# A pre-norm attention layer on one core: layer norm statistics from the loaded blocks instead of a second load, and another order at the end of the last slice

## The chip, the cores and the metric

The kernel runs on one core of a Trainium2 chip. The metric is the device time in microseconds (us) of one execution. Before the change the median of three runs is 2884.72 us (2884.47 to 2885.43). The engines are named as in the profile: PE is TensorE, with PEld for its weight loads; DVE is VectorE, ACT is ScalarE, POOL is GpSimd and SP is SyncE, which issues nearly all transfers (DMAs).

## The reference

```python
h = jnp.maximum(_layernorm(x, axis=-1), 0.0)          # x: (128, 128, 768), eps 1e-5
x = x + _L0_gnn_ref(h, adj, Wq, bq, Wk, bk, Wv, bv, beta)

# in _L0_gnn_ref: 12 heads of 64
q = _split_heads(input_graph @ Wq + bq)                # k and v alike
scores = jnp.einsum('bhqd,bhkd->bhqk', q, k) / jnp.sqrt(HD)
scores = scores + beta * adj_e                         # adj_e = adj[:, None]
scores = jnp.where(adj_e > 0, scores, -9e15)
probs = jax.nn.softmax(scores, axis=-1)
out = jnp.einsum('bhqk,bhkd->bhqd', probs, v)
```

There are 128 graphs of 128 nodes with 768 features. Each graph is normed row by row, projected to queries, keys and values, and attends within itself where its adjacency is positive. The attention's output is added to x. All is float32.

## The kernel before

The graphs go through the core in 32 groups (G = 0 to 31) of four. For each group the kernel makes three projections, called slices: `qk0` (queries and keys of heads 0 to 5), `v` (all values) and `qk1` (queries and keys of heads 6 to 11). A slice is not a plain product of blocks: the list `PRODUCTS` names 15 products of sums of activation blocks (`A..`, `S..`) with sums of weight blocks (`B..`, `T..`), and what each adds to or takes from which output block. A product is one call of `product` (L355) with eight matmul instructions, 16 records in the trace. Each product belongs to one of four chains (a, b, c, d); a chain has one PSUM bank, in which its products accumulate one after another. After each product the bank is read, by ACT (L392) where it is the first for its output block, otherwise by a DVE addition (L396 for q and k, L382 and L387 for v). The next product of the same chain writes that bank again, so it has to wait until it has been read. There are eight banks in a queue `free`; `take` and `give` move them in order.

The loop over G writes out by hand what else is done after which product: `then(n, f)` puts f behind product n of the slice that is being built. In this way the attention of one group runs inside the slices of its own and the next group. `scores` (L406) follows product 1 of a slice: it makes three pairs of score blocks in six banks, each read by DVE with the bias (L421) and then exponentiated by ACT (L424). `attend` (L443) multiplies with the values (L452), takes reciprocals of the sums, and divides (L429 to L436); POOL adds x (L457) and SP stores. The order on each engine's queue is set by a scheduler from these calls; `issue_after` (in `behind`, `behind_scores` and others) forbids it to place a step ahead of a named one.

The next group G+1 is prepared meanwhile. Its x is loaded in blocks of 32 nodes by 192 features (`load_x`, L151), into tiles that come free when the previous group's blocks have been transposed (`to_hT`, L310, L315), which happens in the qk1 slice. ACT norms the blocks in place (`norm`, L304, L308) during the v slice, with a scale `rstd` and a shift for each.

Layer norm statistics come in two ways. In group 0's and group 1's loop turns (so for groups 1 and 2) `stats` (L225, L230) takes them from the x blocks on DVE, 16 per group. A row's 768 features lie on four partitions there, so `moments_1` (L235) sums the means over partitions with two small matmuls on PE (L241), four records, in a bank of its own, then DVE makes deviations (L244 to L248), `moments_2` (L251) does the same for the variances (L255 to L260), and POOL takes the power -1/2 and the shift (L262, L264). The bank is held for three products. From G = 2 on, that is for groups 3 to 31, the rows are loaded a second time instead, as whole rows in two halves (`load_halves`, L271), into tiles that share their places with `adj` and `adjT`; DVE takes statistics of 384 features (`row_stats`, L283, L284), `row_moments` (L286) finishes them with two DVE and two POOL instructions and sends them to the blocks' partitions by 16 transfers of 1 KB (L299). `load_adj` (L324), `bias_1` (L332) and `bias_2` (L348) make the bias from adjacency: a transposition, a mask, a product, a fill of the tile on POOL, a predicated copy, a square on ACT and a maximum.

The last group's qk1 slice has its own order of products (`LAST`) and half blocks of attention (`scores_half`, L460; `attend_half`, L481; arguments: head pair, then which two graphs), named here (5,0), (4,0), (3,0), (3,1), (5,1), (4,1). `scores_half` loads x for the residual, makes the scores (L472), bounds and biases them (L476) and exponentiates (L479). `attend_half` multiplies with the values (L489) and hands on `store`: division, residual addition (L497) and the store (L499). For (4,1) the `store` waits in the list `stores` until `over` (L742) has been computed from all divisors; `over` decides, by a small matmul (L744) and a reduction (L745), if the slow general path has to run.

Of the kernel before, what the change touches and what calls it, by code (L numbers as in the profile page):

```python
# [17 lines left out]
P = 128  # L18
# [96 lines left out]
def direct(ctx, tc, x, adj, wq, bq, wk, bk, wv, bv, beta, out, bad):  # L115
# [153 lines left out]
    rows = {}  # L269

    def load_halves(G, g):  # L271

        for h in range(2):
            t = rows[G, g, h] = work.tile([P, VH], F32, tag=("adj", "adjT")[h], name=f"half_{G}_{g}_{h}", bufs=1)
            nc.sync.dma_start(t, x[G * GRP + g, :, h * VH:(h + 1) * VH])

    def row_stats(G, g):

        if g == 0:
            rows[G] = stat.tile([P, GRP, 2, nc.vector.BN_STATS_DIM], F32, tag="strow", name=f"strow_{G}", bufs=1)  # L280
            rows[G, "mv"] = stat.tile([P, GRP, nc.vector.BN_AGGR_DIM], F32, tag="mvrow", name=f"mvrow_{G}", bufs=1)
        for h in range(2):
            nc.vector.bn_stats(rows[G][:, g, h, :], rows[G, g, h])  # L283
        nc.vector.bn_aggr(rows[G, "mv"][:, g, :], rows[G][:, g])  # L284

    def row_moments(G):  # L286

        mv = rows[G, "mv"]
        ve = stat.tile([P, GRP], F32, tag="verow", name=f"verow_{G}", bufs=1)
        nc.vector.tensor_scalar(ve, mv[:, :, 1], EPS, None, op0=ALU.add)  # L290
        mean = stat.tile([P, GRP], F32, tag="meanrow", name=f"meanrow_{G}", bufs=1)
        nc.vector.tensor_scalar(mean, mv[:, :, 0], -1.0, None, op0=ALU.mult)
        t = stat.tile([P, 2, GRP], F32, tag="row2", name=f"row2_{G}", bufs=1)
        nc.gpsimd.tensor_tensor(t[:, 0], ve, nhalf.to_broadcast([P, GRP]), ALU.pow)
        nc.gpsimd.tensor_tensor(t[:, 1], mean, t[:, 0], ALU.mult)
        to = stat.tile([P, NB, 2, GRP], F32, tag="block2", name=f"block2_{G}", bufs=1)
        for b in range(NB):
            for a in range(NB):
                nc.sync.dma_start(to[a * SQ:(a + 1) * SQ, b], t[b * SQ:(b + 1) * SQ])  # L299
        for g in range(GRP):  # L300
            for b in range(NB):
                rstd[G, g * NB + b], shift[G, g * NB + b] = to[:, b, 0, g:g + 1], to[:, b, 1, g:g + 1]

# [156 lines left out]
    def scores_half(G, oc, r):  # L460
# [14 lines left out]
        for i in range(2):  # L475
            nc.vector.scalar_tensor_tensor(e[:, i], ps[i][:, 0:2 * N].rearrange("p (g n) -> p g n", g=2), SCORE_CAP * ISCALE, biasT[G][:, 2 * r:2 * r + 2, :],  # L476
                                           op0=ALU.min, op1=ALU.add)
            give(ps[i])
            nc.scalar.activation(e[:, i], e[:, i], AF.Exp, scale=1.0 / ISCALE)  # L479

    def attend_half(G, oc, r):  # L481
# [11 lines left out]
        def store():  # L493
            divide()
            give(bank)
            t = xo[G, oc, r]
            nc.vector.tensor_add(t, t, o.rearrange("p (b j) d -> p b (j d)", j=2))  # L497
            g0 = G * GRP + 2 * r
            nc.sync.dma_start(out[g0:g0 + 2, :, oc * P:(oc + 1) * P].rearrange("g n d -> n g d"), t)  # L499

        if r == 1 and oc == 4:
            stores.append(store)
        else:
            store()
# [52 lines left out]
    def rows_1(g):  # L557

        t = xg[0, g].rearrange("p b f -> p (b f)")
        s = stat.tile([P, 2, nc.vector.BN_STATS_DIM], F32, tag="strow_0", name=f"strow0_{g}", bufs=2)  # L560
# [5 lines left out]
        mv = stat.tile([P, nc.vector.BN_AGGR_DIM], F32, tag="mvrow_0", name=f"mvrow0_{g}", bufs=2)  # L566
        nc.vector.bn_aggr(mv, s)
        ve = stat.tile([P, 1], F32, tag="verow_0", name=f"verow0_{g}", bufs=2)
# [77 lines left out]
    early, raw = [], []  # L646
    for G in range(NG):
# [4 lines left out]

        def behind(f, *args):

            with tc.issue_after(added[G].ins):
                return f(*args)
# [4 lines left out]
        if G + 1 < NG:  # L661
            for g in range(GRP):
                then(6, lambda g=g: load_x(G + 1, g, (nc.sync,)))
                if G == 1:
                    then(11 + g, lambda g=g: behind_scores(stats, G + 1, g))
                elif G:
                    then((0, 5, 8, 11)[g], lambda g=g: load_halves(G + 1, g))
                    then((4, 7, 10, 13)[g], lambda g=g: behind(row_stats, G + 1, g))
            if G > 1:
                raw = []  # L670
                then(14, lambda: raw.append(load_adj(G + 1)))
                then(14, lambda: row_moments(G + 1))
# [17 lines left out]
        if G + 1 < NG:  # L690
            got = []
            at = 3 if G else 5
            for g in range(GRP):
                if not G:
                    then(g, lambda g=g: stats(G + 1, g))
                then(at + 5 + g, lambda g=g: behind(norm, G + 1, g) if G > 1 else norm(G + 1, g))
            if G < 2:
                then(at, lambda: got.extend(moments_1(G + 1, 0, GRP * NB)))
                then(at + (3 if G else 2), lambda: moments_2(G + 1, 0, GRP * NB, *got[:2]))
            if G:  # L700
                then(8, lambda: got.append(behind(bias_1, G + 1, raw.pop()) if raw else bias_1(G + 1, load_adj(G + 1))))
                then(12, lambda: bias_2(G + 1, got[-1]))
# [29 lines left out]
        for at, f, *args in (  # L732
            (0, load_xo, 0), (0, load_xo, 1), (0, load_xo, 2), (0, attend, 0), (2, attend, 2), (4, attend, 1),
            (9, scores_half, 5, 0), (10, scores_half, 4, 0), (11, attend_half, 5, 0), (12, scores_half, 3, 0),
            (12, attend_half, 4, 0), (13, scores_half, 3, 1), (13, attend_half, 3, 0), (14, scores_half, 5, 1),
            (14, attend_half, 3, 1), (14, scores_half, 4, 1), (14, attend_half, 5, 1), (14, attend_half, 4, 1),
        ):
            then(at, lambda f=f, args=args: f(G, *args))
        slice_of(G, "qk1", todo, LAST)
# [138 lines left out]
```

## Time and profile before

| what | value |
| --- | --- |
| median of 3 runs | 2884.72 us |
| the profiled execution's own time | 2884.47 us |
| its span, first to last instruction | 2882.7 us |
| granted TensorE clock | 0.999 |
| start of the qk1 slice of groups 1, 2, 3 | 164.79, 253.96, 343.13 us |
| L283, statistics of half rows (DVE) | 232 instructions, 118.2 us, 549 ns each |
| L230, statistics of a block (DVE) | 40 instructions, 344 ns each |
| L294, power for a group's rows (POOL) | 29 instructions, 1017 ns each |
| L262, power for a group's blocks (POOL) | 2 instructions, 2908 ns each |
| L457, residual addition 128x512 (POOL) | 189 instructions, median 1.27 us |
| L497, residual addition 128x256 (DVE) | 6 instructions, 423 ns each |

A timeline line gives start and duration in us, engine, line of the kernel, operation, the tile written and those read, the shapes and the number of records; in brackets the idle time before it and what ended that. Matmul records overlap each other, so the distance from one start to the next says what a matmul costs the queue, and its duration does not.

### The profile page before, as it was taken

The numbers are of one execution on the slowest core, as the hardware profiler recorded it, in microseconds if no ns is written. First come the engines' busy times: TensorE is split into PE (matmuls) and PEld (weight loads), VectorE is DVE, ScalarE is ACT, GpSimd is POOL, SyncE is SP. The second block draws the span as 40 slices with busy tenths as digits, with TensorE's granted clock in tenths as the row PEclk, the third lists the DMA queues.
The fourth block names the chain that finished last, engine by engine and source line by source line (L and its number), as shares of the span: only waits on it lengthen the run. The fifth ranks groups of instructions, "written<-read, shape, count | busy, mean of one in ns | idle before, by whom it ended". The sixth has DMA issues, their size and how long they took to land.

```text
span 2882.7 us, 81559 instructions
## 1 busy us (share of the span) xinstructions
PE 2872.4 (100%) x35330; PEld 2014.5 (70%) x35330; DVE 1955.9 (68%) x4511; ACT 806.5 (28%) x1750; POOL 316.9 (11%) x304
## 2 busy tenths in 40 slices
PE   9999999999999999999999999999999999999999
PEld 7666677666677676776667766677666677666776
DVE  7866666666666666666766666666666666666665
ACT  2422322232222323313232132322223222322221
POOL 1111111111011010110101101011101111110110
PEclk9999999999999999999999999999999999999999
DMA  6222233222232222322223322233222232222311
GB/s 167 77 62 76 58 84 87 73 71 67 75 88 80 64 74 68 87 86 63 76 65 86 90 60 82 60 85 88 69 75 62 80 88 75 69 70 72 88 41 39
DMA packets 413467, 218.31 MB, mean 76 GB/s; under 512 B 110384, under 2 KB 412720, under 8 KB 413104
## 3 DMA queue, kind: packets, MB, share of 16 engines
q1 hardware_dynamic: 411232, 212.66, 26.8%
q8 instruction: 277, 4.54, 0.6%
q10 hardware_dynamic: 1872, 0.40, 0.1%
q14 instruction: 86, 0.70, 0.1%
HBM read 162.14 MB, written 50.33 MB: 74 GB/s over the span
## 4 chain that ended last, share of the span: by engine, by line
PE 99%; DVE 1%; issue 0%; POOL 0%; POOLq 0%
PE bank L371 85%; PE bank L417 6%; PE bank L452 6%; PE bank L533 1%; PE bank L595 0%; DVE A L315 0%; DVE qk_T L206 0%; DVE qk L396 0%; DVE S L321 0%; DVE e L421 0%; PE bank L472 0%; PE bank L489 0%; PE bank L584 0%; DVE e L476 0%; DVE xo L497 0%
## 5 line engine op out<-in xcount | busy, mean ns | idle before, releaser
L371 PE MATMUL bank<-S,qk_T 128*64 128x256 f32 x7056 | 822.5, 379 | 0.8 <-ACT qk L392 0.8
L396 DVE TENSOR_TENSOR qk<-qk,bank 128x512 f32<-128x512 f32 x630 | 426.6, 677 | 411.8 <-PE bank L371 406.3
L371 PEld LDWEIGHTS bank<-S,qk_T 128*64 128x64 f32 x7056 | 503.8, 137 | 256.1 <-ACT e L424 5.2
L392 ACT ACTIVATE qk<-bank,bqk 128x256 f32<-128x256 f32 x756 | 315.8, 469 | 1149.3 <-PE bank L371 962.8
L457 POOL TENSOR_TENSOR xo<-xo,o 128x512 f32<-128x512 f32 x189 | 253.5, 1342 | 2075.2 <-DVE o L436 1777.9
L371 PE MATMUL bank<-S,qk_B 128*64 128x256 f32 x4032 | 478.2, 379 | 1.0 <-DVE qk L396 1.0
L371 PE MATMUL bank<-A,qk_T 128*64 128x256 f32 x4032 | 478.6, 379 | 0.4 <-DVE qk L396 0.4
L371 PE MATMUL bank<-v_T,S 128*64 128x256 f32 x3584 | 421.8, 380 | 0.0
L424 ACT ACTIVATE e<-e 128x512 f32<-128x512 f32 x378 | 227.8, 628 | 642.8 <-DVE e L421 641.8
L371 PEld LDWEIGHTS bank<-A,qk_T 128*64 128x64 f32 x4032 | 284.3, 137 | 137.0 <-DVE qk L396 0.5
L387 DVE TENSOR_TENSOR v<-v,bank 128x512 f32<-128x512 f32 x320 | 219.8, 687 | 232.6 <-PE bank L371 230.8
L371 PEld LDWEIGHTS bank<-S,qk_B 128*64 128x64 f32 x4032 | 278.6, 137 | 128.9 <-DVE qk L396 1.4
L371 PEld LDWEIGHTS bank<-v_T,S 128*64 128x64 f32 x3584 | 254.7, 137 | 130.4 <-issue 5.7
L421 DVE SCALAR_TENSOR_TENSOR e<-bank,biasT 128x512 f32<-128x512 f32 x378 | 231.7, 682 | 109.1 <-PE bank L417 109.1
L371 PE MATMUL bank<-v_B,S 128*64 128x256 f32 x2048 | 243.2, 379 | 0.0
L371 PE MATMUL bank<-v_T,A 128*64 128x256 f32 x2048 | 237.9, 379 | 0.0
L308 ACT ACTIVATE x<-x,block 128x192 f32<-128x192 f32 x464 | 217.3, 535 | 39.9 <-DMA block<-row 39.1
L452 PEld LDWEIGHTS bank<-v,e 128*64 128x64 f32 x6048 | 208.6, 138 | 27.3
L315 DVE STREAM_TRANSPOSE A<-x 128x256 f32<-128x256 f32 x378 | 211.8, 612 | 4.0 <-ACT x L308 4.0
L452 PE MATMUL bank<-v,e 128*64 128x65 f32 x6048 | 208.3, 221 | 0.0
L382 DVE TENSOR_TENSOR v<-bv_b,bank 128x512 f32<-128x512 f32 x192 | 131.8, 687 | 105.2 <-PE bank L371 105.2
L371 PEld LDWEIGHTS bank<-v_B,S 128*64 128x64 f32 x2048 | 147.1, 137 | 73.9
(90 smaller groups left out, 1603.6 us busy)
## 6 DMA issues: line engine op xcount, KB each, us to landing
x<-in_x_dram SPq DMA_DIRECT2D x504, 96.0 KB, 2.6
xo<-in_x_dram SPq DMA_DIRECT2D x189, 256.0 KB, 3.0
out_dram<-xo SPq DMA_DIRECT2D x189, 256.0 KB, 2.6
half<-in_x_dram SPq DMA_DIRECT2D x232, 192.0 KB, 2.8
adj<-in_adj_dram SPq DMA_DIRECT2D x128, 64.0 KB, 3.0
block<-row SPq DMA_DIRECT2D x464, 1.0 KB, 1.7
qk_T<-in_L_gnn_Wq_dram SPq DMA_DIRECT2D x10, 128.0 KB, 3.7
qk_T<-in_L_gnn_Wk_dram SPq DMA_DIRECT2D x10, 128.0 KB, 3.8
```

The costliest lines, as they stand in the source:

```text
L308: nc.scalar.activation(t, t, AF.Relu, bias=shift[G, n], scale=rstd[G, n])
L315: last = nc.vector.transpose(t[:, :, g * N:(g + 1) * N].rearrange("p c (b i) -> p c b i", i=SQ), src)
L371: nc.tensor.matmul(p[q:q + HD, i, :], lhs[:, q:q + HD], rhs, start=(first and i == 0 and c == 0), stop=(c == 1), skip_group_check=True)
L382: added[G] = nc.vector.tensor_tensor(o4, bias[:, None, :, :].to_broadcast([P, 2, 4, HD]), p.rearrange("p g (h d) -> p g h d", d=HD), ALU.a ...
L387: added[G] = nc.vector.tensor_tensor(o, o, got, ALU.add if sign > 0 else ALU.subtract)
L392: nc.scalar.activation(t[:, i, :], p[:, i, :], AF.Identity, bias=bqk[:, i, oc:oc + 1], scale=float(sign))
L396: added[G] = nc.vector.tensor_tensor(t, t, p, ALU.add if sign > 0 else ALU.subtract)
L417: nc.tensor.matmul(ps[oc, i][k:k + HD, g * N:(g + 1) * N], t[r, 1, at][:, k:k + HD], t[r, 0, at], start=True, stop=True)
L421: taken[0] = nc.vector.scalar_tensor_tensor(e, ps[oc, i].rearrange("p (g n) -> p g n", g=GRP), SCORE_CAP * ISCALE, biasT[G], op0=ALU.min, ...
L424: nc.scalar.activation(e, e, AF.Exp, scale=1.0 / ISCALE)
L452: nc.tensor.matmul(pa[q:q + HD, 2 * g + i, :], es[G, oc, i][:, 2 * r + g, q:q + HD], vt[G, "v", r, h // 4][:, 4 * g + h % 4, :], start=Tru ...
L457: nc.gpsimd.tensor_add(t, t, o.rearrange("p a (b j) d -> p (a b) (j d)", j=2))
```

## The change

In the main loop the second way of taking statistics is removed: `load_halves`, `row_stats`, `row_moments` and the ordering helper `behind` go. All groups from 3 on now take `stats`, `moments_1` and `moments_2` like groups 1 and 2. In the loop's text `stats` stand behind products 11 to 14 of the qk0 slice, without an order after the scores; `moments_1` stand behind product 3 and `moments_2` behind product 6 of the v slice; the adjacency is loaded where `bias_1` is called. As built, the scheduler places the 16 `bn_stats` of group G+1 in the qk1 slice of group G-1, between its last additions, and the bias's DVE work in the following qk0 slices.

In the last slice the scores of (5,1) stand behind product 13 instead of 14; the divisions, additions and stores of all three `r == 1` blocks go into `stores`; that of (3,1) is taken out first and ordered after the last score sums; those of (5,1) and (4,1) follow `over`. The additions of (3,1) and (5,1) go to POOL. Some tags of the first group's statistics tiles are renamed.

```diff
-    def load_halves(G, g):
...
-    def row_stats(G, g):
...
-    def row_moments(G):
...
+            taken[0] = nc.vector.scalar_tensor_tensor(e[:, i], ps[i][:, 0:2 * N].rearrange("p (g n) -> p g n", g=2),
+                                                      SCORE_CAP * ISCALE, biasT[G][:, 2 * r:2 * r + 2, :],
+                                                      op0=ALU.min, op1=ALU.add)
...
-            nc.vector.tensor_add(t, t, o.rearrange("p (b j) d -> p b (j d)", j=2))
+            engine = nc.gpsimd if r == 1 and oc != 4 else nc.vector
+            engine.tensor_add(t, t, o.rearrange("p (b j) d -> p b (j d)", j=2))
...
-        if r == 1 and oc == 4:
+        if r == 1:
             stores.append(store)
...
-                    then((0, 5, 8, 11)[g], lambda g=g: load_halves(G + 1, g))
-                    then((4, 7, 10, 13)[g], lambda g=g: behind(row_stats, G + 1, g))
-            if G > 1:
-                raw = []
-                then(14, lambda: raw.append(load_adj(G + 1)))
-                then(14, lambda: row_moments(G + 1))
+                    then(11 + g, lambda g=g: stats(G + 1, g))
...
-                then(at + 5 + g, lambda g=g: behind(norm, G + 1, g) if G > 1 else norm(G + 1, g))
-            if G < 2:
-                then(at, lambda: got.extend(moments_1(G + 1, 0, GRP * NB)))
-                then(at + (3 if G else 2), lambda: moments_2(G + 1, 0, GRP * NB, *got[:2]))
+                then(at + 5 + g, lambda g=g: norm(G + 1, g))
+            then(at, lambda: got.extend(moments_1(G + 1, 0, GRP * NB)))
+            then(at + (3 if G else 2), lambda: moments_2(G + 1, 0, GRP * NB, *got[:2]))
             if G:
-                then(8, lambda: got.append(behind(bias_1, G + 1, raw.pop()) if raw else bias_1(G + 1, load_adj(G + 1))))
-                then(12, lambda: bias_2(G + 1, got[-1]))
+                then(8, lambda: got.append(bias_1(G + 1, load_adj(G + 1))))
+                then(12, lambda: bias_2(G + 1, got[2]))
...
-            (12, attend_half, 4, 0), (13, scores_half, 3, 1), (13, attend_half, 3, 0), (14, scores_half, 5, 1),
+            (12, attend_half, 4, 0), (13, scores_half, 3, 1), (13, attend_half, 3, 0), (13, scores_half, 5, 1),
             (14, attend_half, 3, 1), (14, scores_half, 4, 1), (14, attend_half, 5, 1), (14, attend_half, 4, 1),
         ):
             then(at, lambda f=f, args=args: f(G, *args))
+        then(14, lambda: behind_scores(stores.pop(0)))
```

## The prediction

> **What bounds the kernel now.** I read the page first: which engine is full, and the chain that ended last.
>
> ```profile
> PE 2872.4 (100%) x35330; PEld 2014.5 (70%) x35330; DVE 1955.9 (68%) x4511; ACT 806.5 (28%) x1750; POOL 316.9 (11%) x304
> ...
> PE 99%; DVE 1%; issue 0%; POOL 0%; POOLq 0%
> ```
>
> TensorE (PE) is busy all the span and is 99% of the chain. The table of waits, asked for PE between 170 and 2780 us, is empty: from group 2 on PE waits for nobody. The same slice start recurs every 89.17 us (164.79, 253.96, 343.13), up to the last group. So a DMA or VectorE instruction that goes away in these groups brings nothing by itself, and one that PE has to issue more is paid in full.
>
> Next, PE's timeline. Group 1 of the kernel before still takes its statistics in the way that the change gives to all groups: two pairs of tiny matmuls in the v slice (L241, L255; a pair is two instructions, four records).
>
> ```profile
> 142.06 3.67 PE L371 MATMUL bank<-v_T,S 128*64 128x256 f32 x32
> 145.57 0.26 PE L241 MATMUL bank<-st,mean 128*64 128x32 f32 x4
> 145.66 1.93 PE L371 MATMUL bank<-v_B,S 128*64 128x256 f32 x16
> 147.41 1.90 PE L371 MATMUL bank<-v_T,S 128*64 128x256 f32 x16
> 149.14 1.90 PE L371 MATMUL bank<-v_B,S 128*64 128x256 f32 x16
> 150.87 0.26 PE L255 MATMUL bank<-dev,mean 128*64 128x32 f32 x4
> 150.95 1.93 PE L371 MATMUL bank<-v_T,S 128*64 128x256 f32 x16
> 152.71 1.90 PE L371 MATMUL bank<-v_T,A 128*64 128x256 f32 x16
> ```
>
> And the same stretch one group later, where the statistics come from the second load:
>
> ```profile
> 231.46 3.67 PE L371 MATMUL bank<-v_T,S 128*64 128x256 f32 x32
> 234.97 1.90 PE L371 MATMUL bank<-v_B,S 128*64 128x256 f32 x16
> 236.69 1.90 PE L371 MATMUL bank<-v_T,S 128*64 128x256 f32 x16
> ```
>
> First column start, second duration. What counts is start to start: a product takes 1.73 us. With a pair ahead of it, it takes 147.41 - 145.57 = 1.84, and 152.71 - 150.87 = 1.84.
>
> Last, the timeline of the end, after the last product has started at 2871.18:
>
> ```profile
> 2873.01 0.67 PE L472 MATMUL bank<-qk 64*64 64x128 f32 x16
> ...
> 2876.33 0.42 ACT L479 ACTIVATE e<-e 128x256 f32<-128x256 f32 x1 [0.19 <-DVE e L476]
> ...
> 2877.49 0.15 DVE L429 TENSOR_SCALAR sm<-bank 128x4 f32<-128x4 f32 x1
> ...
> 2878.18 0.41 DVE L436 TENSOR_TENSOR o<-bank,sm 128x256 f32<-128x256 f32 x1
> ...
> 2878.70 0.42 DVE L497 TENSOR_TENSOR xo<-xo,o 128x256 f32<-128x256 f32 x1
> ...
> 2879.15 0.37 SPq L499 DMA_DIRECT2D out_dram<-xo  x1
> ```
>
> Here VectorE (DVE) and ScalarE (ACT) hold the end: exponentials, last divisors, division, residual addition, the last store.
>
> **Part 1: PE pays for the moments.** Groups 3 to 31, 29 of them (L294 ran 29 times), each get two pairs. A pair costs 1.84 - 1.73 = 0.11 us. The whole v slice says the same: 164.79 - 135.73 = 29.06 in group 1 against 253.96 - 225.13 = 28.83 in group 2, 0.23 us. 29 x 0.23 = **+6.7 us**. Reading error 0.01 us a group: 6.4 to 7.0. Nothing hides it, since PE never waits.
>
> The TensorE page of the Trainium skill ("TensorE: Matmul & The Clock Gate", Back-to-back issue gap) would count small matmuls by an issue floor of about 25 ns: by it eight records make 0.2 us a group and 5.8 us in all, an estimate. The page's section on LDWEIGHTS gives columns / 1.2 ns, 53 ns for 64 columns: were these loads not hidden, the estimate would be 12.4 us. The row lies near the first.
>
> **Part 2: what goes from SyncE and what DVE does instead.** Off per group: eight half loads, 16 transfers of 1 KB, on DVE L283, L284, L290 and L292 (118.2, 24.2, 4.7 and 4.7 us over 29 groups: 5.2 us each). On: 16 block statistics (L230), a run of four 1.13 us, so 4.5, and six tiny reductions and sums of 0.16 to 0.20, 1.1. On balance +0.4 us on an engine that is 68% busy. GpSimd's power goes from 1.0 (128x4) to 2.9 us (128x16), off the path as in group 1: norms there started at 155.40 and sixteen at about 0.45 ended near 162.6, 2 us ahead of the next slice. The bank that the moments hold for three products was held in group 1 too, with no wait on PE. The adj load (four transfers) moves up on SyncE's queue by more than a slice ahead of its transposition, so no wait for it is new.
>
> **Part 3: where the statistics land.** In the built order they do not stay beside the qk0 slice. All 16 stand inside the qk1 slice of the group before, and the bias (transposition of adj, mask, product, predicated copy, maximum; 3.2 us) moves from the v slice to the qk0 slice, behind its scores. The qk1 slice has this DVE load now:
>
> ```profile
> 254.00:282.70 28.70, 28.70 (x340) 20.06 (x338) 22.94 (x56) 5.03 (x12) 4.20 (x3) 1.00 0.31 85
> ```
>
> (fourth number: DVE busy, 22.94 of 28.70 us.) With 4.5 more it is at 96%, and its queue is in order, so a statistic that waits for its x holds all behind it. I went through that slice in the new order on group 2's clock. The first four (x_0) come at 268.9; x_0 landed by 267.8. The first of x_1 comes at 273.0; its last piece is issued about 271.0, behind the store of xo, and lands 2.7 us later: DVE waits 0.7 us. Then the qk addition of product 9 is at 274.0 (now 273.38), of 10 at 276.6, of 11 at 279.0 to 279.6 (now 278.18), of 14 at 285. PE needs an addition done when the next product of the same chain overwrites its bank: product 12 at 277.48, 13 at 279.21, 14 at 280.94. The tightest is 11 before 14, with 1.3 us to spare. The last statistics (x_3) wait again: the store of xo_1 comes 1.6 us later, x behind it lands about 287.2, and the next scores are read at 288.4 instead of 287.36. Behind them the copy waits for GpSimd's fill (0.52) and the maximum for the square on ACT (0.63); the additions of the qk0 slice run up to 3 us late, but the banks are next written at 298.6 and later and the first attend there is at 295.95. DVE is level again by 300. So I take 0 for PE's stall, with ends 0 and 0.25 us a group (7 us) for the case that the 1.3 us is eaten. A gain is excluded: PE has no wait to lose.
>
> **Part 4: the end.** The score block (5,1) goes ahead of the last product: that starts 0.7 later (scores and switch, 0.62 + 0.60 less the 0.51 of the old succession), its qk addition ends 2874.5 instead of 2873.8, and the last scores start at 2874.6 instead of 2874.23. But on DVE they no longer wait for two other score additions, a division and an addition: their sums start at 2875.25 instead of 2875.22 and 2875.88, the second ends 2876.0 instead of 2876.29, and the last divisor is read at 2877.2 instead of 2877.49: -0.27. Then it is given back. Behind the test `over` now stand two divisions, not one: (5,1), the reduction of `bad`, (4,1), and then the last addition, which ends near 2879.27 instead of 2879.12: +0.15. The addition of (5,1) is on GpSimd. A 128x512 one took 1.27 and a 128x16 operation 0.22; between them 128x256 is 0.73, so it ends about 2879.1 and its store is issued to 2879.5. The last store stands behind it on SyncE's queue and starts near 2879.55 instead of 2879.15: **+0.4 us**. Ends: -0.3 (divisor gain kept whole, stores no matter) and +1.0 (GpSimd at the full 1.27). The addition of (3,1), also on GpSimd, is done near 2877.2, long before. That of (3,0) now stands behind a score sum, 0.3 later; the tile of (4,1) is loaded into its buffer by 2877.2 and needed at 2878.8.
>
> The page "GPSIMD Engine Reference" of the skill (Engine selection) speaks against the move: it puts two-input elementwise work on GpSimd at about twice VectorE's time. From the 0.42 of the row that makes 0.84, an estimate, and the end would be 0.1 later than by the interpolation.
>
> **Sum.** 6.7 + 0 + 0.4 = +7.1 us. The profiled execution took 2884.47 (span 2882.7 and 1.8 around it), 0.25 under the median 2884.72. On its own time 2891.6, on the median 2891.8; I say 2891.7.
>
> **Rivals.**
> 1. VectorE becomes the bound of the qk1 slice. For it: 96% load, two waits for x in front of additions that PE needs. Against: 1.3 us to spare at the tightest place, and 3.1 idle us at the slice's start (258 to 261) that keep delays from adding up. It decides once the pieces of x_1 land 1.3 us later than I have them; then each 0.1 us costs 2.9 us. With 0.25 us a group 2899; with 0.5 us 2906.
> 2. Not slower by a measurable amount: the pairs cost only their own start-to-start, 145.66 - 145.57 = 0.09 us, because the product behind runs at its pace. For it: that gap stands in the trace. Against: the product behind took 1.75 in the same rows. 58 x 0.09 = 5.2, with the end 5.6: 2890.3. Since 0.2% (5.8 us) is about what can be told from no change here, this decides below 0.093 us a pair.
> 3. The relief of SyncE and the DMAs pays. PE's empty table of waits leaves no place for it; it would need a wait that the profile hides, and 2884 or less.
>
> **How the numbers follow.** The forecast (no stall, 0.11 a pair) has 0.78, its own range 2890.8 to 2892.7 (the median with 6.4 - 0.3 and 7.0 + 1.0). Rival 1 has 0.13, rival 2 0.08, rival 3 0.01. The range goes down to rival 2 with an end that costs nothing (5.2 us: 2889.9, taken as 2889.8) and up to a stall of 0.18 us a group, 2897; it leaves out the larger part of rival 1. Slower by over 0.2%: forecast and rival 1, 0.91 less a little for the forecast's lower end, 0.9. Within: 0.09. Faster: 0.01.
>
> **What the changed profile would show.** L241 and L255 (under new line numbers) with 128 records each instead of 12; v slices of 29.06 us in every group; a period of 89.40 instead of 89.17; PE's waits still empty between groups 2 and 30 (rival 1: PE waiting for a DVE addition of qk, at every product 14 of a qk1 slice); DVE waits on the DMA of x, under 2 us a group; the last store issued about 0.4 us later against the last product. I am wrong if the period is not 89.40 within 0.05, or if the end after the last product differs by over 1 us.

## The result, and the profile after

The changed kernel takes 2894.78 us (median of 6 runs, 2894.47 to 2896.14). The kernel before, run beside it, takes 2884.99 us (6 runs, 2884.47 to 2885.43). The change makes the kernel slower: the ratio is 1.0035, with a 95% interval of 1.0022 to 1.0048. That is 9.8 us more, where the prediction's sum was 7.1. The profiled execution took 2894.62 us, with a span of 2892.8, so it can be set beside the profiled execution of before (span 2882.7): 10.1 us to explain.

The page of the kernel after, its busy times, its memory traffic and its chain of waits:

```profile
PE 2879.0 (100%) x35562; PEld 2020.3 (70%) x35562; DVE 1961.3 (68%) x4741; ACT 801.5 (28%) x1750; POOL 372.4 (13%) x306
...
HBM read 116.53 MB, written 50.33 MB: 58 GB/s over the span
...
PE 97%; issue 1%; DVE 1%; DMA 0%; POOL 0%; ACT 0%; SPq 0%; ACTq 0%; POOLq 0%; DVEq 0%
```

PE has 232 records more, which is 29 groups times eight. The core reads 45.6 MB less than before (162.14 MB on the page of before), and nothing comes back for it: PE is still 97% of the chain.

PE's timeline in the v slice of group 2 of the kernel after, the stretch that the prediction showed without the moments:

```profile
231.87 3.67 PE L336 MATMUL bank<-v_T,S 128*64 128x256 f32 x32
235.37 0.26 PE L241 MATMUL bank<-st,mean 128*64 128x32 f32 x4
235.46 1.93 PE L336 MATMUL bank<-v_B,S 128*64 128x256 f32 x16
237.22 1.90 PE L336 MATMUL bank<-v_T,S 128*64 128x256 f32 x16
...
240.67 0.26 PE L255 MATMUL bank<-dev,mean 128*64 128x32 f32 x4
240.76 1.93 PE L336 MATMUL bank<-v_T,S 128*64 128x256 f32 x16
242.51 0.82 PE L336 MATMUL bank<-v_T,A 128*64 128x256 f32 x6
```

From the start of a pair to the start of the second product behind it are 237.22 - 235.37 = 1.85 and 242.51 - 240.67 = 1.84 us, where a product alone takes 1.73. The qk1 slices of groups 1, 2 and 3 start at 165.20, 254.60 and 344.00: the period is 89.40 instead of 89.17.

The table of waits of the kernel after between 170 and 2780 us, PE's and then VectorE's (what waited, for whom, us in total, times, the longest):

```profile
PE bank L336 <- DVE qk L361: 0.2, 1, 0.2
```

```profile
DVE st L230 <- DMA x<-in_x_dram: 74.6, 69, 2.7
DVE bm L315 <- ACT adjT L311: 20.3, 29, 0.8
DVE biasT L305 <- POOL biasT L304: 17.9, 29, 0.6
```

PE's table was empty and has one entry now. VectorE's waits for x are new, about 2.6 us a group.

The end of the kernel after, from the last score sums on:

```profile
2883.31 0.76 DVE L441 SCALAR_TENSOR_TENSOR e<-bank,biasT 128x256 f32<-128x256 f32 x2 [0.27 <-PE bank L437]
2883.83 0.72 ACT L445 ACTIVATE e<-e 128x256 f32<-128x256 f32 x2 [2.03 <-DVE e L441]
...
2885.22 0.16 DVE L394 TENSOR_SCALAR sm<-bank 128x4 f32<-128x4 f32 x1 [0.47 <-PE bank L455]
...
2885.92 0.41 DVE L401 TENSOR_TENSOR o<-bank,sm 128x256 f32<-128x256 f32 x1
...
2886.40 0.40 DVE L401 TENSOR_TENSOR o<-bank,sm 128x256 f32<-128x256 f32 x1
2886.47 0.72 POOL L464 TENSOR_TENSOR xo<-xo,o 128x256 f32<-128x256 f32 x1 [1.11 <-DVE bad L703]
2886.84 0.63 DVE L464 TENSOR_TENSOR xo<-xo,o 128x256 f32<-128x256 f32 x1
```

The two divisions behind `over` start at 2885.92 and 2886.40. GpSimd adds (5,1) in 0.72 us, and VectorE's last addition, beside it, takes 0.63 us instead of 0.42. The stores of (5,1) and (4,1) are issued at 2887.22 and 2887.65, and they land 3.58 and 3.36 us later. The transfers of the stores from 2875 us on, before and after (us from issue to landing):

```profile
DMA to landing us min/median/max: 1.8/1.8/1.8
```

```profile
DMA to landing us min/median/max: 1.8/2.0/3.6
```

**Where the 10.07 us of the two profiled executions lie.** I took the start of the first product of each slice in both traces and subtracted.

| part | us |
| --- | --- |
| up to the start of group 2, all of it by the end of group 0's qk1 slice | 0.41 |
| 29 v slices, 0.233 each | 6.77 |
| qk1 slices: 0.44 in group 5, 0.18 in group 8, 0.06 to 0.11 and less in a few others | 0.81 |
| qk0 slices | 0.0 |
| end, up to the issue of the last store | 0.51 |
| end, landing of the last store, 3.36 instead of 1.81 | 1.55 |

The lines add up to 10.05; the other 0.02 us lie behind the last landing. The first line is not put down to the change: in the profiled executions of the experiments that leave the moments' matmuls alone this part lies between 0.1 and 0.7 us above before's, also where the main loop takes its statistics as before (0.34, 0.53, 0.59 and 0.69 in four such kernels).

VectorE in the qk1 slice of group 2 of the kernel after, the stretch that the prediction showed of before (the fourth number is VectorE's busy time), and its statistics in the same stretch:

```profile
254.60:283.30 28.70, 28.70 (x338) 20.06 (x336) 24.21 (x64) 5.03 (x12) 4.18 (x3) 1.00 0.30 83
```

```profile
L230 DVE BATCH_NORM_STATS2 st<-x 128x6 f32<-128x192 f32 x9 | 2.8, 342 | 0.8 <-DMA x<-in_x_dram 0.8
```

Nine of the 16 statistics run in the slice, and the rest behind it. The nine add 2.8 us to before's 22.94, so 1.5 us of other work have moved out of the slice as well.

**The stall of group 5.** VectorE's and PE's lines in that qk1 slice of the kernel after:

```profile
544.26 0.36 DVE L230 BATCH_NORM_STATS2 st<-x 128x6 f32<-128x192 f32 x1 [2.44 <-DMA x<-in_x_dram]
...
549.44 0.68 DVE L361 TENSOR_TENSOR qk<-qk,bank 128x512 f32<-128x512 f32 x1
...
550.17 1.08 PE L336 MATMUL bank<-S,qk_T 128*64 128x256 f32 x8 [0.22 <-DVE qk L361]
```

A transfer of x landed after 4.37 us, not after about 2.7 (of 504 transfers of x, 28 took over 4.0 us, 4.7 at most). VectorE stood 2.44 us at the statistic, its queue kept order, the addition of qk came late and PE waited for its bank.

What made that transfer late can be looked for among the transfers' records. On the same DMA engines runs a queue whose kind the profile calls "instruction", in packets of 16 KB that take about 1.0 us each. The page of the kernel after (packets, MB, share of the 16 engines' time):

```profile
q8 instruction: 279, 4.57, 0.7%
```

The late transfer was issued at 539.86, and such a packet ran from 541.82 to 542.74. Of the 504 transfers of x, 107 have one in the stretch from 1.0 to 2.2 us after their issue. They land after 3.50 us in the median, the other 397 after 2.49, and 26 of the 28 over 4.0 us are among the 107. No experiment moved these packets, so this is a finding of the records and not a tested cause.

### The profile page after: what moved, and what is told of

It is laid out like the page before. It is cut to its first block, busy times and chain, and to the rows that moved or that the text cites. A ratio compares the mean times of both kernels' runs of the same rounds, so it can differ in the third digit from the quotient of the medians.

```text
span 2892.8 us, 81360 instructions
## 1 busy us (share of the span) xinstructions
PE 2879.0 (100%) x35562; PEld 2020.3 (70%) x35562; DVE 1961.3 (68%) x4741; ACT 801.5 (28%) x1750; POOL 372.4 (13%) x306
## 4 chain that ended last, share of the span: by engine, by line
PE 97%; issue 1%; DVE 1%; DMA 0%; POOL 0%; ACT 0%; SPq 0%; ACTq 0%; POOLq 0%; DVEq 0%
PE bank L336 84%; PE bank L417 6%; PE bank L382 6%; PE bank L501 1%; DMA x<-in_x_dram 0%; ACT x L273 0%; POOL rstd L262 0%; DVE S L286 0%; PE bank L437 0%; PE bank L455 0%; PE bank L241 0%; DVE qk L361 0%; PE bank L255 0%; PE bank L552 0%; DVE qk_T L206 0%
## 5 line engine op out<-in xcount | busy, mean ns | idle before, releaser
L273 ACT ACTIVATE x<-x,shift,rstd 128x192 f32<-128x192 f32 x504 | 224.3, 533 | 350.1 <-POOL shift L264 350.1
L230 DVE BATCH_NORM_STATS2 st<-x 128x6 f32<-128x192 f32 x504 | 154.4, 344 | 76.8 <-DMA x<-in_x_dram 76.4
```

The source lines that it names most:

```text
L230: nc.vector.bn_stats(st[G][:, g * NB + b, :], xg[G, g][:, b, :])
L273: nc.scalar.activation(t, t, AF.Relu, bias=shift[G, n], scale=rstd[G, n])
```

## The experiments

All times are medians of five or more runs (four in experiment 6) and are compared with the kernel before as it ran beside them (medians of 2885.00 to 2885.18 from 9 to 26 runs). These medians repeat within some 0.5 us. The intervals of the ratios are about 3 to 4 us to each side, so differences of a microsecond between kernels rest on the traces as well as on the medians, and I say where they don't agree.

**1. The statistics alone.** The changed kernel with the end of before:

```diff
-            (12, attend_half, 4, 0), (13, scores_half, 3, 1), (13, attend_half, 3, 0), (13, scores_half, 5, 1),
+            (12, attend_half, 4, 0), (13, scores_half, 3, 1), (13, attend_half, 3, 0), (14, scores_half, 5, 1),
...
-            engine = nc.gpsimd if r == 1 and oc != 4 else nc.vector
-            engine.tensor_add(t, t, o.rearrange("p (b j) d -> p b (j d)", j=2))
+            nc.vector.tensor_add(t, t, o.rearrange("p (b j) d -> p b (j d)", j=2))
...
-        if r == 1:
+        if r == 1 and oc == 4:
...
-        then(14, lambda: behind_scores(stores.pop(0)))
```

> The changed kernel with its last slice put back as before: only the statistics are changed. Theory A (the change is two separate prices: PE's moments and VectorE's late additions in the main loop, 8.0 us up to the last product in the traces; the end of the last slice, 2.1 us): this run is 7.5 to 8.2 us slower than before, 2.0 less than the change, the period is 89.40 us, and the last store lands 1.8 us after its issue. Rival B (the slow landing at the end comes with the new main loop, not with the new end): 9.3 us or more slower, and the last stores land 3 us or more after their issue.

Measured: 2892.51 us, ratio 1.0026 (1.0016 to 1.0036), +7.3 us. In the trace the v slices take 6.77 more, the qk1 slices 0.73, and the last store lands in 2.00 us. The time is just under the 7.5 that the first theory began at. Three quarters of the change's cost are the statistics.

**2. The end alone.** The kernel before with the changed end (the same edit the other way round).

> The kernel before with the last slice of the change: only the end is changed. Theory A (two stores issued within 0.5 us of each other take 3.4 to 3.6 us to land instead of 1.8, whenever it happens): 2.0 us slower than before, 0.5 of it before the last store is issued and 1.5 in its landing. Rival B (the landing was a chance of one execution): 0.4 to 0.6 slower, last landing 1.8 to 2.2 us.

Measured: 2887.16 us, ratio 1.0007 (0.9998 to 1.0016), +2.0 us, by itself within the interval. Its trace repeats what the changed kernel's end shows: the last two stores are issued 0.44 us apart and land 3.93 and 3.83 us later.

```profile
DMA to landing us min/median/max: 1.8/2.0/3.9
```

**3. The statistics placed later.** The changed kernel, in which the statistics of every group are ordered after the score sums of the qk0 slice, as group 2's are:

```diff
-                    then(11 + g, lambda g=g: stats(G + 1, g))
+                    then(11 + g, lambda g=g: behind_scores(stats, G + 1, g))
```

> The changed kernel, but the block statistics of every group are ordered after the scores, as those of group 2 are: they fall in the qk0 slice, after x has landed. Theory A (about 0.8 us of the loss are PE stalls in the qk1 slices of a few groups, where a statistic holds VectorE's queue until its x has landed): PE waits for no addition of qk between groups 2 and 30, every period is 89.40, VectorE's waits for x fall from 76 us to under 10, and the time is 0.6 to 1.0 us under that of the change. Rival B (these stalls have another cause, such as VectorE's load alone): the same stalls, or others in the qk0 slice, and no gain.

Measured: 2893.97 us, ratio 1.0031 (1.0019 to 1.0043), +8.8 us, 0.8 below the changed kernel. VectorE's waits for x are gone, PE's table of waits is empty again, and no qk1 slice is longer than before. So the 0.8 us of the qk1 slices come from the place of the statistics, and there is room for them elsewhere.

**4. Both corrections.** Experiment 3's edit and before's end together.

> The changed kernel with the end of the kernel before, and with the statistics of every group issued behind the score additions of the qk0 slice, as those of group 2 are. Theory A: with both corrections only PE's moments are left, 29 x 0.233 = 6.8 us, no slice of another kind is longer than before, and the last store lands in 1.8 to 2.0 us: 6.5 to 7.3 us over the kernel before. Then the change's 9.8 us divide into 6.8 for the moments, 0.8 for statistics in the qk1 slice and about 2 for the end. Theory B: the qk1 slice is not where the rest was lost (or the moments cost more where the statistics come late): as with the end alone undone or more, 7.3 to 8.5 us over.

Measured: 2891.80 us (11 runs), ratio 1.0023 (1.0014 to 1.0032), +6.6 us. In the trace the v slices take 6.77 more, the qk1 and qk0 slices 0.00, and the end is before's (landings 1.83 and 1.82). PE's timeline of this kernel:

```profile
235.62 0.26 PE L241 MATMUL bank<-st,mean 128*64 128x32 f32 x4
235.71 1.93 PE L336 MATMUL bank<-v_B,S 128*64 128x256 f32 x16
237.46 1.90 PE L336 MATMUL bank<-v_T,S 128*64 128x256 f32 x16
```

This is the part that no arrangement tried here takes away: two pairs a group on an engine that never waits.

**5. The moments' matmuls twice.** Each pair of the changed kernel issued two times, with the same result:

```diff
-        for q in range(0, P, HD):
+        for q in 2 * (0, HD):
```

and the same in `moments_2`.

> The changed kernel with each of the moments' matmul pairs issued twice into the same place (60 more pairs in 30 groups, 32 columns each; the first group's half-size ones too). Theory A (by the record): each extra pair costs 0.087 to 0.113 us, 5.3 to 6.9 us over the change, and the gap from the first small matmul to the next product grows from 0.09 to 0.17. Rival B (fixed price of the switch): under 2 us over the change.

Measured: 2902.38 us, ratio 1.0060 (1.0046 to 1.0073), +17.2 us, 7.5 over the change. PE's timeline:

```profile
236.49 0.38 PE L241 MATMUL bank<-st,mean 128*64 128x32 f32 x8
236.69 1.93 PE L336 MATMUL bank<-v_B,S 128*64 128x256 f32 x16
238.45 1.90 PE L336 MATMUL bank<-v_T,S 128*64 128x256 f32 x16
```

Two pairs cost 238.45 - 236.49 - 1.73 = 0.23 us, and the v slice grows by 0.467 a group instead of 0.233, 6.8 us more over 29 groups. Group 2's pairs, doubled too, add 0.24 in the trace, and group 1's and the first group's half-size ones were doubled as well. What then remains of the 7.5, somewhat more than expected, is no larger than the medians' repeat. The price goes by the pair, 0.117 us. The second pair is not cheaper than the first, so the 0.117 is not a fixed toll for breaking into the products.

**6. A pair as one instruction over 128 columns.** The changed kernel, half as many matmuls for the moments, each twice as wide:

```diff
-        for q in range(0, P, HD):
-            nc.tensor.matmul(pm[G, lo][q:q + HD, 0], mean8.rearrange("p a i -> p (a i)")[:, q:q + HD],
-                             halves(G, lo, hi, 1), start=True, stop=True)
+        nc.tensor.matmul(pm[G, lo][:, 0], mean8.rearrange("p a i -> p (a i)"), halves(G, lo, hi, 1),
+                         start=True, stop=True)
```

and the same in `moments_2`.

> The changed kernel with each pair of moments' matmuls (two instructions with 64 columns of the mean matrix each) made one instruction with 128 columns. Theory A (PE pays by the record, about 0.022 us each, and 0.025 us once for the switch): a pair costs 0.06 to 0.08 instead of 0.11 us, the time is 2 to 3 us under that of the change. Rival B (PE pays a fixed price for leaving the stream of products, whatever stands there): no difference beyond 0.5 us. Rival C (the 128-column weight load is not hidden): 2 us slower than the change or more.

Measured: 2917.40 us, ratio 1.0111 (1.0096 to 1.0127), +32.3 us, 22.6 over the change, the direction of rival C. The v slice grows by 0.98 us a group, 0.49 for each instruction instead of 0.117 for a pair. The timeline, weight loads (PEld) and matmuls:

```profile
236.71 0.30 PEld L240 LDWEIGHTS bank<-st,mean 128*128 128x128 f32 x2 [0.39 <-issue]
236.72 0.41 PE L240 MATMUL bank<-st,mean 128*128 128x32 f32 x2
237.06 1.95 PE L333 MATMUL bank<-v_B,S 128*64 128x256 f32 x16
```

The weight load stands 0.39 us "in issue": it waits for nothing that the profile shows, and it starts only at 236.71, with its matmul. In the changed kernel the 64-column loads of the same weights have no such gap. The Trainium skill says in "TensorE: Matmul & The Clock Gate", Step-by-step, that PE pulls a weight load ahead of running matmuls when the row groups don't conflict or when it goes to the background buffer. The trace agrees for loads of the products' own width and shows no such pull where the width changes from 64 to 128 columns; why, no run here shows.

**7. The second load fetched twice.** The kernel before, each half load issued twice into the same tile:

```diff
             nc.sync.dma_start(t, x[G * GRP + g, :, h * VH:(h + 1) * VH])
+            nc.sync.dma_start(t, x[G * GRP + g, :, h * VH:(h + 1) * VH])
```

> The kernel before with every half row of the second load fetched twice (8 more transfers of 192 KB per group from group 3 on, 45 MB in all). Theory A (the second load is hidden, so taking it away could bring nothing): within 0.5 us of before and an empty table of PE's waits from 170 to 2780 us. Rival B (SyncE's queue or the transfers have a price): slower than before by 2 us or more.

Measured: 2903.31 us, ratio 1.0055 (1.0041 to 1.0069), +18.2 us. Its five runs scatter more than those of any other kernel here, from 2896.29 to 2906.93. The expectation that transfers cost nothing here fell. The table of waits, PE's and VectorE's line for the halves:

```profile
PE bank L418 <- DVE qk L397: 10.7, 11, 2.1
PE bank L372 <- DVE qk L397: 1.9, 3, 0.7
```

```profile
DVE strow L284 <- DMA half<-in_x_dram: 185.3, 115, 4.3
```

VectorE waits 115 times for a half row, up to 4.3 us (before: 1.7 us in all, 5 times), its queue keeps order, and additions that PE needs come late. That leaves two causes: the doubled transfers and issues themselves, or the landing that VectorE's queue hangs on.

**8. More transfers that nobody waits for.** The kernel before, with a third more bytes and twice the issues for the second load, into a spare part of the tile that nobody reads:

```diff
-            t = rows[G, g, h] = work.tile([P, VH], F32, tag=("adj", "adjT")[h], name=f"half_{G}_{g}_{h}", bufs=1)
+            s = work.tile([P, VH + P], F32, tag=("adj", "adjT")[h], name=f"half_{G}_{g}_{h}", bufs=1)
+            t = rows[G, g, h] = s[:, 0:VH]
             nc.sync.dma_start(t, x[G * GRP + g, :, h * VH:(h + 1) * VH])
+            nc.sync.dma_start(s[:, VH:VH + P], x[G * GRP + g, :, h * VH:h * VH + P])
```

> The kernel before, in which each of the eight half loads of a group is followed by one more load of 128 of its columns into a spare part of the same tile that nobody reads: eight more issues on SyncE's queue in each group and a third more of the bytes of the second load, 15 MB in all. When the half loads were fetched twice into the same tile, the time rose by 18.2 us, and it is open whether the queue and the bandwidth made that or the chain behind the landing (statistics that wait on VectorE's in-order queue and hold the additions behind them). Theory A (the chain): the statistics wait for the first load alone, the landing is later by 0.1 to 0.4 us only, and the time is within 1 us of before, 2884.2 to 2886.2. Theory B (SyncE's queue and the transfers): a third of the bytes and all the issues give 6 to 18 us, 2891 to 2903.

Measured: 2884.95 us (11 runs), ratio 1.0000 (0.9991 to 1.0009), the same as before. VectorE's line for the halves:

```profile
DVE strow L285 <- DMA half<-in_x_dram: 11.2, 18, 1.5
```

The halves land a little later, VectorE waits 11.2 us instead of 1.7, and PE's table of waits stays empty. Doubling SyncE's issues for these loads costs nothing, which agrees with nothing coming back when the change takes them away. So it is not the issues that cost 18 us in experiment 7. Its waits point to landings that became late for the queue behind them; whether the doubled bytes (here a third more) or the second write into the same tile made them late was not separated.

**9. The other queue.** The changed kernel, with the store of (5,1) issued by ACT:

```diff
-            nc.sync.dma_start(out[g0:g0 + 2, :, oc * P:(oc + 1) * P].rearrange("g n d -> n g d"), t)
+            (nc.scalar if (oc, r) == (5, 1) else nc.sync).dma_start(out[g0:g0 + 2, :, oc * P:(oc + 1) * P].rearrange("g n d -> n g d"), t)
```

> The changed kernel with the store of (5,1) issued by ScalarE's queue instead of SyncE's; the last store no longer stands behind it. Theory A (two stores in flight at the same time delay each other's landing in the DMA engines or memory): the last store is issued 0.2 to 0.4 us earlier, but both still land 3 us or more after their issue; 0.2 to 0.5 us under the change. Rival B (the landing is slow because both are in one queue): landing back to 1.8 us, 1.5 to 2 us under the change.

Measured: 2894.97 us, ratio 1.0035 (1.0021 to 1.0049), as the changed kernel. The last two stores are issued 0.27 us apart on two queues and land 3.58 and 3.63 us later. The late landing is not made by SyncE's queue. The 0.2 to 0.5 us that I had looked for from the earlier issue are not to be seen.

**10. An end with both divisions ahead of the test.** The kernel before with the changed end, and (5,1) also finished ahead of `over`:

```diff
         then(14, lambda: behind_scores(stores.pop(0)))
+        then(14, lambda: stores.pop(0)())
```

> The kernel before with the last slice of the change, but the division, addition and store of (5,1) stand ahead of the test over, too, so that only (4,1) follows it. Theory A (the new end loses by the second division behind the test and by two stores close together): the last store is issued 0.2 to 0.5 us earlier against the last products than in the kernel before and lands in 1.8 us; the time is 0.0 to 0.5 us under before. Rival B (the earlier scores bring nothing, since the last divisor waits for something else): 0.3 us slower than before or more.

Measured: 2885.05 us, ratio 1.0000 (0.9991 to 1.0009), -0.1 us. The last three stores are issued at 2877.72, 2878.41 and 2879.47, and all land in 1.8:

```profile
DMA to landing us min/median/max: 1.8/1.8/1.8
```

Less its later start (0.34) the last store is issued no earlier than before's. So this order mends what the change does to the end and gains nothing; no kernel here beats the kernel before.

**11. The last two stores further apart, twice.** First, the changed kernel with the division of (4,1) made two times:

```diff
             divide()
+            if (oc, r) == (4, 1):
+                divide()
             give(bank)
```

> The changed kernel, in which the division of (4,1) is made twice, so that the residual addition of (4,1) and the last store come one more division later (0.40 to 0.45 us by its rows). Open is why the last two stores of the changed kernel land 3.58 and 3.36 us after their issue, where the last stores of the kernel before land after 1.81. Theory A: because they are issued within 0.44 us of each other, whatever they hold and whichever queue issues them. In the main-loop run with both divisions ahead of the test, gaps of 0.69 and 1.06 us left every landing at 1.83. With a gap of about 0.85 both land in 1.8 to 2.0 us again, and the time is 1.55 - 0.42 = 1.1 us below the changed kernel's, 2893.7. Theory B: it is the late end itself, not the gap: the landings stay at 3.3 to 3.6, and the time rises by the 0.4 us, 2895.2.

Second, the changed kernel with the addition of (5,1) on VectorE:

```diff
-            engine = nc.gpsimd if r == 1 and oc != 4 else nc.vector
+            engine = nc.gpsimd if r == 1 and oc == 3 else nc.vector
```

> The changed kernel, with the residual addition of (5,1) on VectorE again (that of (3,1) stays on GpSimd). VectorE then makes after the test: division, addition, division, addition. The store of (5,1) is issued from about 2886.8 instead of 2887.2 on the changed kernel's clock; the last addition stands one addition later but no longer runs beside GpSimd (0.63 to 0.42), so it ends about 2887.7 and the last store is issued within 0.3 us of the changed kernel's. Theory A (closeness of the two stores makes them land late): the gap is about 0.85 us, both land in 1.8 to 2.0 us, and the time is 1.2 to 1.6 us below the changed kernel's: 2893.2 to 2893.6. Theory B (it is not the gap): within 0.3 us of the changed kernel, 2894.5 to 2895.1.

Measured: 2896.12 us for the first (ratio 1.0039, 1.0026 to 1.0053) and 2894.97 for the second (1.0036, 1.0023 to 1.0050). Neither gave the 1.1 to 1.6 us. In the first the gap became 0.52 us and not 0.85: VectorE's last addition no longer overlaps GpSimd's and takes 0.42 instead of 0.63 us, and the last store no longer stands behind the other's issue, so the extra division of 0.45 us moved it by 0.09 only. The landings are 3.23 and 3.14, late as before. In the second the gap is 0.79 and the landings are 1.92 and 2.71. Its end, from the last product on, is 0.64 us shorter than the changed kernel's, but its qk1 slices lost 1.1 us in that execution instead of 0.8, and the median did not move. In the first they lost 1.7 us. The stall of the qk1 slices thus differs from kernel to kernel with the same main loop, 0.6 to 1.7 us; whether anything but the scatter of x's landings is behind that stays open.

All gaps and landings of the last two stores, from the records of the profiled executions:

| kernel | gap between issues, us | landings, us |
| --- | --- | --- |
| changed, ACT issues one (9) | 0.27 | 3.58, 3.63 |
| changed | 0.43 | 3.58, 3.36 |
| changed, statistics later (3) | 0.43 | 3.52, 3.29 |
| one instruction over 128 columns (6) | 0.43 | 3.80, 3.68 |
| moments' matmuls twice (5) | 0.43 | 3.27, 3.15 |
| changed end alone (2) | 0.44 | 3.93, 3.83 |
| division twice (11) | 0.52 | 3.23, 3.14 |
| addition on VectorE (11) | 0.79 | 1.92, 2.71 |
| both divisions ahead (10) | 1.06 (and 0.69 ahead of it) | 1.83, 1.81 (and 1.83) |
| second load fetched twice (7) | 1.52 | 1.83, 1.90 |
| statistics alone (1) | 1.53 | 1.83, 2.00 |
| both corrections (4) | 1.54 | 1.83, 1.82 |
| more transfers (8) | 1.55 | 1.84, 1.81 |
| before | 1.55 | 1.83, 1.81 |

Every pair at 0.52 us and below lands late, on one queue or two and with either main loop; every pair at 1.06 and above does not. Between them 0.69 and 0.79 differ. So closeness goes with the late landing; that it is the cause is not shown, because something else goes with it too, and sorts more of the cases: the instruction packets met in group 5's stall.

In all 14 traces a 16 KB packet of q8 starts 1.67 to 2.03 us after `bad`, the outcome of the test, has been written; it takes 0.9 to 1.8 us. In the six kernels with one division behind `over` the last store is issued 0.39 to 0.40 us after `bad`. The packet then starts 1.36 to 1.64 us behind the issue, when nearly all of the store's own packets have started, and the landing is 1.81 to 2.00. In the eight with two or three divisions there the last store is issued 1.02 to 1.27 us after `bad`, the packet starts 0.43 to 0.66 us behind the issue, and the landing is 2.71 to 3.83. The pair at 0.79, which the gap does not sort, falls in line: the packet starts 1.38 us behind the issue of its first store, which lands after 1.92, and 0.59 behind that of its second, which lands after 2.71. And closeness is not needed: in experiments 1 and 4 a store earlier in the last slice, with no other store within 2.8 us, was issued while such a packet ran and landed after 2.85 and 2.56; in the other kernels the same store landed after 1.8 to 2.4. So the records point to the second division behind the test, which moves the last stores into these packets, rather than to the gap. No run moved one without the other, and the cause of the late landing stays open.

## Why the prediction was right, point by point

- **Part 1, +6.7 us for the moments: right.** Measured 6.76 to 6.77 in the v slices of every kernel with the new statistics (but for experiments 5 and 6, which alter the pairs), and 6.6 us as a time where it stands alone (experiment 4). Two timeline rows of group 1 had the price. By records it is 0.117 / 4 = 29 ns each. The estimate from the skill's issue floor of 25 ns, given in the prediction, came out at 5.8, 1.0 too low. The other one, 12.4 for weight loads that are not hidden, doesn't hold for loads of the products' width; experiment 6 shows 0.49 instead of 0.117 us where the width differs.
- **Part 2, nothing comes back from SyncE and the DMAs: right.** PE had no wait to lose, and experiment 8 shows the other direction: twice the issues and a third more bytes cost nothing either. Experiment 7 is the limit of that: there landings came late for VectorE's queue.
- **Part 3, 0 for PE's stall: the size was off by 0.8 us.** The mechanism is the one given as rival 1: statistics that wait for x hold VectorE's queue. The spare time was rightly read as 1.3 us: in group 5 VectorE stood 2.44 us where the prediction had 0.7 for group 2, 1.7 more, and the slice lost 0.44, so 1.3 were absorbed. But I put one typical landing (2.7 us) into it. The landings scatter up to 4.7 us, and group 5's was 1.7 later than that typical one. With 29 groups the tail is met a few times, so the term should have been some tenths to 1 us, not 0. The load was misjudged the other way: only 9 of the 16 statistics run inside the qk1 slice of group 2, and other work moved out too, so VectorE is busy 24.2 of 28.7 us there, 84% and not 96%. That fits the stall's being rare; no run tests it. VectorE waits 2.6 us a group for x, not under 2.
- **Part 4, +0.4 us for the end: right up to the issue, and a term was missing behind it.** On before's clock (the changed kernel's less 7.99, its lead at the start of the last slice) the last scores start at 2874.62 (predicted 2874.6), the last divisor is read at 2877.23 (2877.2), GpSimd's addition ends at 2879.20 (2879.1) and the last store is issued at 2879.66 (2879.55). GpSimd's 0.72 to 0.75 us stands at the interpolated 0.73, not at twice VectorE's 0.42. Missing was, first, that VectorE's addition beside it takes 0.63 instead of 0.42. The skill's "GPSIMD Engine Reference", Specifications, has GpSimd share its SBUF interfaces with VectorE and names contention with VectorE instructions of two SBUF inputs; the row agrees, and in both kernels of experiment 11, where no GpSimd addition runs beside it, VectorE's takes 0.42 to 0.43 again. Missing was, second and larger, the landing: I ended the sum at the issue of the last store and took its 1.81 us as given. It became 3.36, +1.55. The prediction had named an end that differs by over 1 us as a sign of its being wrong. On before's clock the last store lands 2.06 us later (0.51 + 1.55) where 0.4 was forecast, so by that sign the step failed, while the other sign, the period of 89.40, held.
- **Rival 2 (a pair at 0.09 us) fell**: experiment 5 gives 0.117 for each pair added. **Rival 3 (the relief pays) fell** with Part 2.

By times, the 9.8 us of the change are 6.6 for the moments (experiment 4), 0.7 to 1.0 for the place of the statistics (7.3 - 6.6 from experiments 1 and 4, 9.8 - 8.8 from 3) and 2.0 to 2.5 for the end (experiment 2 alone, and 9.8 - 7.3). The total stayed inside the stated range, 2889.8 to 2897, because the two missed terms, 0.8 and 1.55, are small beside its main one; the forecast's own range, 2890.8 to 2892.7, it left. The upper part of the stated range was meant for a stall of PE, and about 0.8 us of the excess is one. The larger part is the landing, which no part of the prediction had, so that the range held it is luck.

## What to carry to other kernels

When PE's table of waits is empty, price a change by the PE records it adds, taken start to start from the timeline, and expect nothing from relief of the other engines. For a wait with spare time behind it, compare the spare time with the tail of the landings and not with their median, since over many groups the tail will be met. Carry the sum of an end through to the landing of the last store, and look at what else the DMA engines move at that time: the stores before it, and the packets of kind "instruction".

## What the runs showed of the hardware that was not expected

- Two stores of 128 KB issued last and 0.27 to 0.52 us apart landed after 3.1 to 3.9 us each, seven kernels out of seven; the last two 1.06 us and more apart landed after 1.8 to 2.0. The late ones also ran beside a 16 KB packet of kind "instruction", the others hardly did (experiment 11). The skill's "DMA: Bandwidth & Descriptors", Latency and other measured facts, says that the memory's access latency rises with load and is most of a transfer's fixed cost; the landings agree in direction, but no run here shows that this is the cause. In the changed kernel four fifths of the two stores' packets had started within 0.94 us of the first, and the last twentieth only 2.0 to 2.5 us after it: some packets were late, not all.
- A transfer of x of 96 KB with a 16 KB packet of kind "instruction" in the stretch from 1.0 to 2.2 us after its issue landed after 3.50 us in the median, without one after 2.49 (107 and 397 transfers of the changed kernel).
- A matmul over 128 columns among matmuls over 64 cost 0.49 us where two over 64 cost 0.117 us, by a weight load that stood 0.39 us in issue.
- A VectorE addition of 128x256 took 0.63 us beside a GpSimd addition of the same size and 0.42 us without it.
